# Attention on a graph: the product that spreads queries to edges, in two float32r halves instead of one fp32 product

## The chip, the cores and the metric

The kernel runs on one core of one Trainium2 chip. The time is the device time of a run in microseconds. The profile shows one execution, taken by the hardware profiler.

## What is computed

Eight layers over a graph of 3,125 nodes and 53,125 edges (sorted by destination), 256 features, each added to the stream x. The change is in the first, a graph attention with 8 heads of 32:

```
q = (nfeat @ Wq.T).reshape(n, HEADS, HEAD_DIM) / SCALING
k = (nfeat @ Wk.T).reshape(n, HEADS, HEAD_DIM)
v = (nfeat @ Wv.T).reshape(n, HEADS, HEAD_DIM)
attn = jnp.einsum('ehd,ehd->eh', k[src], q[dst])
attn = attn + attn_bias
m = jax.ops.segment_max(attn, dst, num_segments=n)
a = jnp.exp(attn - m[dst])
s = jax.ops.segment_sum(a, dst, num_segments=n)
a = a / s[dst]
out = jax.ops.segment_sum(v[src] * a[:, :, None], dst, num_segments=n)
return out.reshape(n, FEAT) @ Wo.T
```

The other layers are a small mixture of experts (it runs beside the attention, node tile by node tile), graph convolutions and larger expert layers.

## The kernel before

Nodes are cut into T = 25 tiles of P = 125. As edges are sorted by destination, the edges of a node tile lie together; each tile gets a window of WC = 18 chunks of 128 edges. A chunk's keys and values are gathered by source node with one indirect DMA from POOL (`gathered`, L1736), six chunks (PC) to a buffer `kv`; there are seven such buffers, three to a tile, and a gather waits for the fifth before it.

The queries of a tile are not gathered. They are a 125x256 matrix `q` (`queries`: two matmuls with `wq`, then a copy on ACT with the scale, L1987), and an edge's query is picked by a matmul: the one-hot matrix of a chunk, nodes by edges (`oht_f`, stationary), times `q` (moving) gives the queries of 128 edges in PSUM (`qx`, L2006 in `logits`). Two chunks fill a PSUM bank, and DVE multiplies the keys in `kv` by it (L2008). After six chunks DVE sums over each head (L2009). The one-hots come as a broadcast row of node numbers in bf16 (`oht`), which DVE compares with the partition's number (L1991); ACT casts them to the type of the matmul (L1995), six chunks at a time, into three buffers, one for each call of `logits` of a tile.

Then follow for each tile: the exponentials and their sums (`sums_of`), the weights (`weights_of`), values times weights on DVE (L2043 in `weighted`) and the sum over the edges of each node, again a matmul with one-hots, in fp32 (`acc`, L2050; its one-hots are cast by ACT at L2048), the division (`normed`), a transpose and the output projection. A loop over tiles interleaves these for three tiles: `now` (logits), `before` (weights, sums, projection) and `after` (loads, one-hots, queries). Between the parts `beside` does a step of the small expert layer (its matmuls are recorded at L300, in the tile `tr` above all).

Loads of a tile (`asked`): the one-hot rows `oht`, the transposed normalized nodes `lt_t` (L1972), and the edge biases `eb_t` (L1974), all on SP's queue, in pools with two buffers.

The order of instructions on each engine is not the order of the code: a planner in the compiler places each instruction by its place in the code and by an estimated time of its inputs, at compile time. At run time each engine takes its instructions in that fixed order, and waits come from semaphores. So an instruction that waits holds back all that stands behind it on its engine.

Later in the kernel the graph convolutions use a product in two float32r halves already: `halves` splits a matrix into a high half (ACT, L2355 or L2358) and the rest (DVE, L2356 or L2359), and `block_pass` multiplies both with a matrix of counts and adds in PSUM (L2418); L2516 transposes both halves by a matmul with an identity.

Of the kernel before, what the change touches and what calls it, by code (L numbers as in the profile page):

```python
# [10 lines left out]
F32 = mybir.dt.float32  # L11
F32R = mybir.dt.float32r
I32 = mybir.dt.int32
BF16 = mybir.dt.bfloat16
AF = mybir.ActivationFunctionType
ALU = mybir.AluOpType
# [6 lines left out]
N, D = 3125, 256  # L23
P, T = 125, 25
# [11 lines left out]
H, HD = 8, 32  # L36
# [12 lines left out]
WC, PC = 18, 6  # L49
# [21 lines left out]
def gnn_ffn_kernel(ctx: ExitStack, tc: tile.TileContext, a, out: bass.AP):  # L71
    nc = tc.nc
# [32 lines left out]
    def move(queue, to, of):  # L105

        queue.dma_start(to[:SPREAD], of[:SPREAD])
        return queue.dma_start(to[SPREAD:], of[SPREAD:])
# [185 lines left out]
    def product(ps, terms, bias=None):  # L294

        last = len(terms) - 1
        if bias is not None:
            nc.tensor.matmul(ps, ones_h[:bias.shape[0], :ps.shape[0]], bias, start=True, stop=False)
        for i, (l, r) in enumerate(terms):
            nc.tensor.matmul(ps, l, r, start=(bias is None and i == 0), stop=(i == last))  # L300
# [1401 lines left out]
    def attention(windows, experts):  # L1702
# [11 lines left out]
        with ExitStack() as es:  # L1714
# [16 lines left out]
            def gathered(at):  # L1731


                kv = rows_tile()
                for c in range(PC):
                    got = nc.gpsimd.indirect_dma_start(  # L1736
                        out=kv[:, c, KO:], out_offset=None, in_=kv_d,
                        in_offset=bass.IndirectOffsetOnAxis(ap=src_i[:, at + c:at + c + 1], axis=0))
                    if len(under_way) > 4:
                        tc.add_manual_dep(got.ins, under_way[-5].ins.name, data_dep, reason="in turn")  # L1740
                    under_way.append(got)
                nc.vector.memset(kv[:, :, KO - 1:KO], 1.0)
                return kv
# [3 lines left out]
            pool = setup.enter_context(tc.tile_pool(name="att_in", bufs=2, reuse_waits="tile"))  # L1747
# [210 lines left out]
            pool = es.enter_context(tc.tile_pool(name="att_s", bufs=2, reuse_waits="tile"))  # L1958
# [6 lines left out]
            def asked(t):  # L1965
                s = Tile()
                s.t, s.kv = t, begun if t == 0 else []
                s.oht = pool.tile([P, WC, 128], BF16, name="oht")
                move(nc.sync, s.oht.rearrange("d c e -> d (c e)"), turned_d[t * WC:(t + 1) * WC, :].rearrange("(o c) e -> o (c e)", o=1)
                     .to_broadcast([P, WC * 128]))  # L1970
                s.lt = pool.tile([128, 2, P], F32, name="lt_t")
                nc.sync.dma_start(s.lt, lt_d[:, :, t, :].rearrange("k f p -> f k p"))  # L1972
                s.eb = pool.tile([128, H, WC], F32, name="eb_t")
                nc.sync.dma_start(s.eb, eb_d[:, t])  # L1974
                return s
# [6 lines left out]
            def queries(s):  # L1982

                ps = psum.tile([P, D], F32, name="sm")
                product(ps, [(s.lt[:, k, :], wq[:, k, :]) for k in range(2)])
                s.q = pool.tile([P, D], F32, name="q")
                nc.scalar.activation(s.q, ps, AF.Copy, scale=float(HD) ** 0.5)  # L1987

            def one_hot_turned(s):
                v = s.oht.rearrange("d c e -> d (c e)")  # L1990
                nc.vector.tensor_scalar(v, v, pcol[:P], None, ALU.is_equal)  # L1991
                s.oht_f = []
                for c0 in range(0, WC, PC):
                    s.oht_f.append(pool.tile([P, PC, 128], F32, name="oht_f", bufs=3))
                    nc.scalar.copy(s.oht_f[-1], s.oht[:, c0:c0 + PC, :])  # L1995
                s.l = pool.tile([128, WC, H], F32, name="l")

            def logits(s, p):

                if p == len(s.kv):  # L2000
                    s.kv.append(gathered(s.t * WC + p * PC))
                kv = s.kv[p]
                for c0 in range(0, PC, 2):
                    ps = psum.tile([128, 2, D], F32, name="qx", bufs=2)
                    for c in range(2):
                        nc.tensor.matmul(ps[:, c, :], s.oht_f[p][:, c0 + c, :], s.q, start=True, stop=True)  # L2006
                    k_ = kv[:, c0:c0 + 2, KO:VO]
                    nc.vector.tensor_mul(k_, k_, ps)  # L2008
                nc.vector.tensor_reduce(  # L2009
                    s.l[:, p * PC:(p + 1) * PC, :],  # L2010
                    kv[:, :, KO:VO].rearrange("p c (h d) -> p c h d", h=H), AX.X, ALU.add)
# [59 lines left out]
            def projected(s):  # L2071
                po = psum.tile([P, D], F32, name="sm")
                product(po, [(s.at[:, k, :], wo[:, k, :]) for k in range(2)])
                nc.vector.tensor_add(x[:, s.t, :], x[:, s.t, :], po)

            now, before = asked(0), None
            one_hot(now)
            one_hot_turned(now)
            queries(now)
            more = experts()  # L2080

# [4 lines left out]
            for t in range(T + 1):  # L2086
                def beside():
                    if t % 4 == 1 and t < 16:
                        next(more_biases[t // 4], None)
                    more.step(t - 1)  # L2090

                after = asked(t + 1) if t + 1 < T else None
                if now:
                    logits(now, 0)
# [10 lines left out]
                if after:  # L2105
                    one_hot_turned(after)
                    queries(after)
                beside()
                if now:
                    logits(now, 1)  # L2110
# [4 lines left out]
                if now:  # L2115
                    logits(now, 2)
# [613 lines left out]
```

## Time and profile before

| | |
|---|---|
| median of 9 runs | 3242.23 us (3238.78 to 3247.43) |
| the profiled execution: its own time, its span | 3237.36 us, 3235.6 us |
| mean granted TensorE clock | 0.973 |
| attention stage, first qx to last tile's `deg` | 98 to 860 us |
| PE / DVE / ACT / POOL busy from 95 to 861 us | 710.0 / 575.8 / 255.3 / 483.4 us |
| DMA share and rate from 95 to 861 us | 0.65, 184 GB/s |
| L2050 acc, 900 records | 215.4 us, 394 ns mean |
| L2008 DVE kv times qx, 225 | 150.7 us, 680 ns mean |
| L1995 ACT cast oht_f, 75 | 828 ns mean |

PE is the matmul engine, PEld its weight loads (they overlap with it), DVE the vector engine, ACT the scalar engine, POOL the engine that issues the gathers, SP the one that issues most other transfers. A matmul's duration of some 380 ns is its latency; matmuls are pipelined, so what one costs is the time from its start to the next one's start. In groups, "xN | a, b | c" is the number, the busy time in us, the mean ns of one, and the idle time of the engine just before them, with what ended it. In waits, "A <- B: a, n, m" is who waited for whom: us in total, times, and the longest.

### The profile page before, as it was taken

The numbers are of one execution on the slowest core, as the hardware profiler recorded it, in microseconds if no ns is written. First come the engines' busy times: TensorE is split into PE (matmuls) and PEld (weight loads), VectorE is DVE, ScalarE is ACT, GpSimd is POOL, SyncE is SP. The second block draws the span as 40 slices with busy tenths as digits, with TensorE's granted clock in tenths as the row PEclk, the third lists the DMA queues.
The fourth block names the chain that finished last, engine by engine and source line by source line (L and its number), as shares of the span: only waits on it lengthen the run. The fifth ranks groups of instructions, "written<-read, shape, count | busy, mean of one in ns | idle before, by whom it ended". The sixth has DMA issues, their size and how long they took to land.

```text
span 3235.6 us, 43324 instructions
## 1 busy us (share of the span) xinstructions
PE 3032.6 (94%) x15467; PEld 2383.2 (74%) x15467; DVE 1739.3 (54%) x4900; ACT 1092.4 (34%) x2135; POOL 705.5 (22%) x664
## 2 busy tenths in 40 slices
PE   6799999999988999999987999979999999999998
PEld 3577777677778898898875888858755555578867
DVE  5577878788798344246671222265532333464683
ACT  3233333333378233233322222234423232332221
POOL 1676676666000000001223333200000000000000
PEclk9799999999999999999998999989999999999999
DMA  6776676776269434444436666554200000033101
GB/s 190 219 214 187 196 197 176 197 201 173 64 229 293 120 95 118 106 113 110 120 105 181 180 201 193 145 150 106 78 12 12 15 20 12 9 106 105 44 1 41
DMA packets 262345, 407.04 MB, mean 126 GB/s; under 512 B 43449, under 2 KB 206951, under 8 KB 262116
## 3 DMA queue, kind: packets, MB, share of 16 engines
q1 hardware_dynamic: 195985, 247.92, 26.4%
q0 software_dynamic: 54832, 143.43, 16.5%
q10 hardware_dynamic: 11299, 12.78, 1.5%
q8 instruction: 126, 2.06, 0.3%
q14 instruction: 103, 0.84, 0.1%
HBM read 333.28 MB, written 70.70 MB: 125 GB/s over the span
## 4 chain that ended last, share of the span: by engine, by line
PE 66%; DVE 6%; ACT 2%; DMA 1%; issue 1%; POOL 0%; POOLq 0%; SPq 0%; ACTq 0%; DVEq 0%
PE agg L2418 22%; PE po L300 19%; PE hid_ps L300 16%; PE tr L300 2%; PE tr L2516 1%; PE tok L1574 1%; PE row L300 1%; DVE hc L316 1%; PE tr L284 1%; DVE hr L316 1%; PE acc L2050 1%; ACT h L1398 1%; DVE an L2307 1%; PE bt L2304 0%; PE bk L2288 0%
## 5 line engine op out<-in xcount | busy, mean ns | idle before, releaser
L2418 PE MATMUL agg<-cnt_f,hp 125*128 125x500 f32 (+1 forms) x3500 | 743.0, 370 | 25.3 <-ACT hp L2358 25.2
L2418 PEld LDWEIGHTS agg<-cnt_f,hp 125*128 125x128 f32 x3500 | 635.0, 189 | 106.6 <-ACT hp L2358 28.3
L1736 POOL DMA_INDIRECT kv<-kv_d,src_w x450 | 472.2, 1049 | 242.2 <-issue 106.5
L2396 ACT CAST cnt_f<-blk 125x500 fp32r<-125x500 bf16 (+1 forms) x435 | 245.5, 565 | 494.5 <-PE agg L2418 472.8
L2396 DVE CAST cnt_f<-blk 125x500 fp32r<-125x500 bf16 (+1 forms) x440 | 186.8, 426 | 232.5 <-PE agg L2418 193.9
L1398 ACT ACTIVATE h<-hid_ps,shift,scale 128x500 f32<-128x500 f32 (+1 forms) x224 | 161.8, 723 | 373.7 <-PE hid_ps L300 371.7
L2006 PE MATMUL qx<-q,oht_f 125*128 125x256 f32 x900 | 250.5, 406 | 26.0 <-DVE kv L2008 21.4
L1405 DVE TENSOR_TENSOR y<-po,wslot 125x256 f32<-125x256 f32 x200 | 84.8, 424 | 340.2 <-PE po L300 339.8
L1626 POOL MEMSET ost<- 128x512 f32 x1 | 0.5, 524 | 1042.6 <-PE row L300 1042.6
L2006 PEld LDWEIGHTS qx<-q,oht_f 125*128 125x128 f32 x900 | 170.2, 200 | 66.3 <-DVE kv L2008 33.1
L2050 PE MATMUL acc<-kv,oh_f 128*125 128x265 f32 x900 | 215.4, 394 | 1.1 <-ACT oh_f L2048 1.1
L300 PE MATMUL po<-wslot,h 128*125 128x256 f32 x800 | 203.0, 386 | 0.1
L300 PEld LDWEIGHTS po<-wslot,h 128*125 128x125 f32 x800 | 145.0, 187 | 75.3 <-ACT h L1398 27.0
L300 PE MATMUL hid_ps<-h,wslot 128*128 128x500 f32 (+1 forms) x448 | 194.5, 557 | 5.3 <-ACT h L1398 1.7
L1257 ACT ACTIVATE hid<-hid_ps,wslot 128x256 f32<-128x256 f32 x208 | 98.3, 474 | 296.2 <-PE hid_ps L300 296.2
L2050 PEld LDWEIGHTS acc<-kv,oh_f 128*125 128x125 f32 x900 | 171.3, 192 | 34.8 <-ACT oh_f L2048 1.5
L1102 POOL DMA_INDIRECT xs_d<-r_l,pos x50 | 59.2, 1184 | 610.6 <-DVE r_l L1098 597.5
L300 PE MATMUL hid_ps<-xe,wslot 128*128 128x256 f32 x832 | 189.1, 385 | 2.2 <-DVE xe L1246 2.2
L300 PE MATMUL hid_ps<-v_rows,wslot 128*128 128x500 f32 (+1 forms) x448 | 186.4, 537 | 0.0
L300 PE MATMUL po<-wslot,hid 128*128 128x256 f32 x832 | 184.5, 378 | 0.0
L2008 DVE TENSOR_TENSOR kv<-kv,qx 128x512 f32<-128x512 f32 x225 | 150.7, 680 | 50.9 <-PE qx L2006 26.8
L300 PEld LDWEIGHTS hid_ps<-xe,wslot 128*128 128x128 f32 x832 | 152.1, 192 | 34.1 <-ACT hid L1257 3.8
(519 smaller groups left out, 4650.6 us busy)
## 6 DMA issues: line engine op xcount, KB each, us to landing
wslot<-in_ex_W SPq DMA_DIRECT2D x52, 1024.0 KB
blk<-an_d SPq DMA_DIRECT2D x60, 546.9 KB
blk<-at_d SPq DMA_DIRECT2D x40, 546.9 KB
blk<-an_d SPq DMA_DIRECT2D x45, 410.2 KB
at_d<-ab SPq DMA_DIRECT2D x25, 683.6 KB
an_d<-an SPq DMA_DIRECT2D x25, 683.6 KB
oht<-turned_d SPq DMA_DIRECT2D x25, 504.0 KB
blk<-at_d SPq DMA_DIRECT2D x30, 410.2 KB
```

The source lines that it names most:

```text
L300: nc.tensor.matmul(ps, l, r, start=(bias is None and i == 0), stop=(i == last))
L316: return nc.vector.tensor_tensor(o.rearrange("p n (d w) -> p n d w", w=2), columns[:, :m].rearrange("p (d w) -> p d w", w=2).unsqueeze(1). ...
L1102: st = nc.gpsimd.indirect_dma_start(out=xs_d, in_=l2[:, i, :].bitcast(I32), in_offset=None, out_offset=bass.IndirectOffsetOnAxis(ap=self.p ...
L1257: nc.scalar.activation(hid[:, m, :], ps[:, :BLK], AF.Gelu, bias=c[:, 4 + m:5 + m])
L1398: nc.scalar.activation(dst[:, m, :c], ps[:, :c], AF.Relu, bias=shift[:, l, col:col + 1], scale=scale[:, l, col:col + 1])
L1405: nc.vector.tensor_add(y, po, bo)
L1736: got = nc.gpsimd.indirect_dma_start(out=kv[:, c, KO:], out_offset=None, in_=kv_d, in_offset=bass.IndirectOffsetOnAxis(ap=src_i[:, at + c: ...
L2006: nc.tensor.matmul(ps[:, c, :], s.oht_f[p][:, c0 + c, :], s.q, start=True, stop=True)
L2008: nc.vector.tensor_mul(k_, k_, ps)
L2050: nc.tensor.matmul(s.acc[:, :D + H + 1], of[:, c, :], kv[:, c, AO:VO], start=(p == 0 and c == 0), stop=(p == 2 and c == PC - 1))
L2396: to(f[:, :n, :], part[0][:, :n, m % MB, :])
L2418: nc.tensor.matmul(ps[f][:, :c], hp[:, m, k, f * 128:(f + 1) * 128], got[:, :c], start=(m == 0 and k == 0), stop=(m == T - 1 and k == 1))
```

## The change

`q` becomes a float32r tile with two parts: ACT writes the scaled query rounded to float32r (12 significant bits), and DVE writes the scaled query less that part, also in float32r. The one-hots are cast to float32r. For each chunk two matmuls with the same stationary one-hots add the two parts in PSUM. The tile `lt_t` has one buffer instead of two.

```diff
@@ asked
-                s.lt = pool.tile([128, 2, P], F32, name="lt_t")
+                s.lt = pool.tile([128, 2, P], F32, name="lt_t", bufs=1)
@@ queries
-                s.q = pool.tile([P, D], F32, name="q")
-                nc.scalar.activation(s.q, ps, AF.Copy, scale=float(HD) ** 0.5)
+                s.q = pool.tile([P, 2, D], F32R, name="q")
+                nc.scalar.activation(s.q[:, 0, :], ps, AF.Copy, scale=float(HD) ** 0.5)
+                nc.vector.scalar_tensor_tensor(s.q[:, 1, :], ps, float(HD) ** 0.5, s.q[:, 0, :].bitcast(F32),
+                                               ALU.mult, ALU.subtract)
@@ one_hot_turned
-                    s.oht_f.append(pool.tile([P, PC, 128], F32, name="oht_f", bufs=3))
+                    s.oht_f.append(pool.tile([P, PC, 128], F32R, name="oht_f", bufs=3))
@@ logits
-                        nc.tensor.matmul(ps[:, c, :], s.oht_f[p][:, c0 + c, :], s.q, start=True, stop=True)
+                        for k in range(2):
+                            nc.tensor.matmul(ps[:, c, :], s.oht_f[p][:, c0 + c, :], s.q[:, k, :],
+                                             start=(k == 0), stop=(k == 1))
```

## The prediction

> **What bounds the kernel now.** I began with the page's busy shares and slices, to see where the changed code runs and which engine is full there.
>
> ```profile
> PE 3032.6 (94%) x15467; PEld 2383.2 (74%) x15467; DVE 1739.3 (54%) x4900; ACT 1092.4 (34%) x2135; POOL 705.5 (22%) x664
> ...
> L2006 PE MATMUL qx<-q,oht_f 125*128 125x256 f32 x900 | 250.5, 406 | 26.0 <-DVE kv L2008 21.4
> ```
>
> The changed product (L2006) has 900 records, though the code asks for 25 tiles x 18 chunks = 450: an fp32 product leaves two records. By its tile view it runs from 98.2 to 836.7 us, which is the attention stage. The windows view says what is full in the middle of that stage (columns: PE, PEld, DVE, ACT and POOL busy, granted clock, DMA share, GB/s).
>
> ```profile
> 300.00:780.00 480.00, 454.17 (x2500) 359.63 (x2499) 375.38 (x790) 170.03 (x355) 320.69 (x304) 0.99 0.68 191
> ```
>
> PE is busy 95% of it, DVE 78%. POOL's 67% leaves out the 0.30 us that its timeline shows between two gathers: 1.25 us each x 18 = 22.5 us of a tile. The `deg` copies that end the tiles follow one another at 29.6 us (147.4 to 859.7 us, 24 steps). PE leads, but two engines stand close behind.
>
> A busy PE is not the same as a PE that decides, so the chain of waits came next. The page's chain breaks off at a gather at 787 us. I walked back by the same rule from the accumulation that ends at 770.5 us, which reaches the start of the program. Of 98.2 to 770.5 us it gives PE 362.0 us (acc 119.6, the neighbouring layer's tr 87.4, qx 80.6), gathers in flight 68.0, their issue on POOL 54.5, DVE 71.5. Before 300 us qx has only 11.7 of that, and the gathers 83. From 787 us on the page's own chain has 5.9 us of qx, and between the two I take 2 us by the same density: **88 us of qx on the chain**, of 900 x 216 ns = 194 us that PE spends on it.
>
> **The rates.** The chain in order of time and the PE timeline give the pace of matmuls that follow one another (start us, us, what):
>
> ```profile
> 475.81 1.89 PE L2006 MATMUL qx<-q,oht_f 125*128 125x256 f32 x8
> 477.54 1.03 PE L300 MATMUL sm<-wo,at 128*125 128x256 f32 x4
> ...
> 1126.34 22.69 PE agg L2418 x100
> 1149.03 1.73 PE tr L2516 x16
> 1150.76 6.96 PE po L300 x32
> 1157.72 17.16 PE agg L2418 x100
> ```
>
> Eight qx records go from 475.81 to 477.54: 216 ns each, so one fp32 product is 432 ns. L2418 is float32r in this kernel and has one record a matmul: 3,500 records for 5 passes x 7 groups x 25 blocks x 4. It takes 227 ns at 500 columns and 172 ns at 376. L2516, float32r at 126 columns, takes 108 ns with a weight load before each.
>
> **The change, part by part.** *Products.* 450 fp32 products of two records become 900 float32r matmuls: no fewer records or weight loads. No row has 256 float32r columns. The line through 500 and 376 (0.444 ns a column) gives 172 - 120 x 0.444 = 119 ns. From below, the 126-column row bounds it (108), from above the 376-column row (172). I take 119, since weight loads that limit at 108 would be covered. PE is relieved of 900 x (216 - 119) = 87 us (40 to 97); the old chain gets shorter by 88 x 97/216 = **39.5 us** (18 to 44). If instructions keep their order and lengths, the chain's saving is all that can be gained, as the rest of this path stays.
>
> The Trainium skill's "TensorE: Matmul & The Clock Gate", section "Back-to-back issue gap", has N/2.4 + 2.5 ns, 109 ns here, and by that the chain would give 43.6 us. The same section expects some 81 ns at 128 columns with weight loads where this trace has 108 at 126, so I stay with the rows.
>
> *The low half on DVE.* 25 new scalar_tensor_tensor of 125x256 out of PSUM. The same operation with the same output stands at L2356:
>
> ```profile
> L2356 DVE SCALAR_TENSOR_TENSOR hp<-v,hp x50: 416/425/428, 1208.8 to 1455.4; 125x256 fp32r<-125x256 f32 x50
> ...
>   ACT hp L2355: 6.3, 23
> ```
>
> 25 x 0.424 = 10.6 us of DVE. It reads SBUF there; L2060, which reads PSUM at this size, has 421 ns, so that is no difference. DVE has 71.5 of 672 us of the chain, 11%, which makes 1 us; all of it on the path makes 10.6. I take 3, since DVE is nearly full in some tiles (28.1 us of 780 to 810).
>
> *Its wait.* The instruction waits for ACT's high half, which waits for PE's product with wq. Until now DVE waited for neither. What is queued behind it on DVE, the kv products that PE and the gathers wait for, waits too. In L2356 the same pair (ACT high, DVE low) lost 6.3 us in 50, 0.13 each: 3.2 us for 25. The upper end is ACT's own wait for that product today:
>
> ```profile
> ACT q L1987 <- PE sm L300: 35.4, 13, 6.5
> ```
>
> 2.7 us a time, for 25 tiles 68 us. I take 3.2, the row of the same pair.
>
> *Casts on ACT.* `oht_f` and the high half are written as float32r instead of fp32. L2396 (ACT, 500 elements to float32r) has 609 ns; with 268 more at 0.83 (the page's 565 ns mean mixes in 375) that is 831, what L1995 takes today. L2355 has 417 ns where L1987 has 384: 25 x 0.03 = 0.8 us on ACT, which is busy 35% of the stage. At nothing; without that cover, 0.8.
>
> *One buffer for `lt_t`.* SP's load of the next tile now waits until the wq product of the tile before has been read. The last such load is issued at 733.3 us and read at 789.9, a lead of 57 us; the product before it ends near 754, which leaves 36 us for a transfer of 125 KB. Behind it in SP's queue stand the `eb_t` load, which already waits on its own buffer (282.6 us for DVE's L2015, in the queue's waits), and the `oht` loads, last issued at 789.4. At nothing; if a delayed `oht` load followed from it, DVE's present wait for such loads (24.6 us in 6) prices one at 4 us.
>
> *The clock.* Between 160 and 800 us the granted clock falls to half seven times, for 3.4 us each. Three of these follow a stretch of over 3.4 us without a matmul; one such pair:
>
> ```profile
> 440.00:443.50 3.50, 0.00 (x0) 0.00 (x0) 2.85 (x7) 1.99 (x4) 3.00 (x2) 1.00 0.37 112
> 444.20:447.60 3.40, 3.02 (x9) 1.66 (x7) 3.40 (x14) 1.40 (x3) 2.55 (x3) 0.51 0.68 187
> ```
>
> Half clock for 3.4 us costs about 1.7 us. A PE that is done sooner waits more: ten more such stretches would be 17 us, none is possible as well; I take two, 3.4 us, as nearer to the seven in 25 tiles of today. "TensorE: Matmul & The Clock Gate", Part 1, ties the drop to an idle window of some 3.4 us, a rule that speaks against relieving an engine that then waits; by it, waits that stay shorter would cost nothing and the sum would be 33 us. Four of the seven drops here follow shorter gaps, so the rule doesn't cover them.
>
> **The sum.** 39.5 - 3 - 3.2 - 3.4 = 30 us off the profiled execution. Its own time was 3237.4 us with a span of 3235.6; the median of nine runs is 3242.2, so 3212 beside the median. What follows the stage starts from its last accumulation (the chain goes on from there through the one-hots of the next stage), so the gain is passed on whole. Over 44 us would take another order of the instructions, and that the planner may give one, since their lengths change, is the largest unknown.
>
> **The rivals.** *PE's whole relief arrives*, because the order adapts: 87 - 7 = 80 us, **3162**. For it: 3.5 us a tile off 29.6 leaves 26.1, above DVE's 23.6 (375.4/480 x 29.6 + 0.4) and POOL's 22.5. Against: today's leader gets to 29.6 only with two followers at 23; three nearly equal ones don't overlap perfectly, and the first 200 us belong to gathers.
>
> *The next one takes over at once*: nothing, **3240** (within 6.5 us of before). For it: six chunks cost DVE three products and a reduction (page: 680 ns; 1746 ns in the by-shape groups), 3 x 0.68 + 1.75 = 3.8 us, and PE 12 x 0.216 = 2.6, so inside the logits DVE is already slower. Against: PE fills the rest of these stretches with acc and tr, and the chain goes through those.
>
> *DVE waits for q* (slower): the wait above at 2.7 us in every tile, 68 us, less the 22% in which DVE idles anyway, 53; 53 + 10.6 - 39.5 = +24, **3266**. It decides from (39.5 - 10.6)/25 = 1.2 us of uncovered wait a tile. For it: ACT really waits so in 13 of 25 tiles, and DVE is strict in its order. Against: the wq product is computed ahead of its use, and the pair at L2355 and L2356 waits little.
>
> That the change doesn't do what it says, a float32r matmul at 256 columns costing 172 ns, leaves 18 - 10 = 8 us, 3234: the upper end of the forecast.
>
> **How the numbers follow.** Forecast (3195 to 3235): 0.45. All of PE's relief (3150 to 3195): 0.17. Nothing: 0.13. Slower by the wait, or by an unlucky new order: 0.25. A measurement of this kernel can tell 0.2%, 6.5 us, from no change. Faster 0.45 + 0.17 = 0.62, same 0.13, slower 0.25. The forecast's own range is 3195 to 3235; that for 8 in 10 reaches half way into both outer cases, 3165 to 3262.
>
> **What would show it.** Right: qx at some 119 ns start to start with 900 records; the tiles' pace at 28.4 us from 300 to 780 us; PE's busy share down, DVE's up. Wrong: qx at 170 ns or more; DVE idle before the new line for ACT over 30 us in all; stretches of half clock in most tiles; a pace under 27 us (the order adapted) or over 29.6.

## The result, and the profile after

| | before | after |
|---|---|---|
| median | 3243.22 us (33 runs) | 3255.82 us (11 runs, 3248.68 to 3261.86) |
| ratio, 95% interval | | 1.0036 [1.0026, 1.0046] |
| profiled execution: own time, span | 3237.36, 3235.6 us | 3252.75, 3250.9 us |
| mean granted clock of the span | 0.973 | 0.950 |
| last `deg` of the attention | 859.9 us | 868.0 us |
| first agg of the next stage | 1036.4 us | 1048.6 us |

The kernel became slower by about 12 us. The page of the changed kernel: busy time of each engine, the granted clock in 40 slices, and the group of the changed product; below it the granted clock of the kernel before.

```profile
PE 3004.1 (92%) x15467; PEld 2378.9 (73%) x15467; DVE 1745.7 (54%) x4925; ACT 1090.4 (34%) x2135; POOL 719.8 (22%) x664
...
PEclk9689899898898999999997999989999999999999
...
L2009 PE MATMUL qx<-q,oht_f 125*128 125x256 f32 x900 | 190.9, 347 | 31.8 <-DVE kv L2012 23.4
```

```profile
PEclk9799999999999999999998999989999999999999
```

PE is less busy, with the same number of records, and qx is cheaper: the forecast's first signs hold. The line of the clock is the one to look at. The second to the eleventh digit are the attention. Before they were a 7 and nine 9s; now they are a 6, five 8s and four 9s. The windows view of the stage before, of the stage after and of its middle (columns: PE, PEld, DVE, ACT, POOL busy, granted clock, DMA share, GB/s):

```profile
95.00:860.00 765.00, 709.41 (x3792) 556.28 (x3792) 574.83 (x1183) 255.27 (x538) 483.36 (x460) 0.95 0.65 184
```

```profile
95.00:868.00 773.00, 677.27 (x3791) 548.16 (x3789) 580.24 (x1205) 253.15 (x538) 496.60 (x459) 0.87 0.65 182
300.00:780.00 480.00, 431.98 (x2479) 350.61 (x2478) 375.78 (x798) 166.19 (x352) 326.82 (x296) 0.91 0.68 188
```

From 300 to 780 us PE is busy 22 us less than before, and the clock is 0.91 where it was 0.99. The other columns moved by 3% at most. The stage, from 95 us to its last `deg`, divided by what PE did (worked out from the trace: PE's busy time, that part of it in stretches of half clock, and the same work counted at full clock, which is busy less half of that part):

```
          stage   PE idle   PE busy   of it at half clock   work at full clock
before    764.9     55.5     709.4          61.3                 678.8
after     773.0     95.7     677.2         164.3                 595.1
```

The change took 84 us of work from PE. Half clock gave back (164.3 - 61.3) / 2 = 51 us, and idle time 40 us, so the stage came out 8 us longer. Half clock came in 26 stretches (201 us in all) after and 10 (69 us) before.

What one drop looks like: PE's timeline (start us, us, what, idle before it and what ended it), and the windows view of the same microseconds, cut where the clock changes.

```profile
360.60 1.19 PE L2009 MATMUL qx<-q,oht_f 125*128 125x256 f32 x8
362.10 0.74 PE L2009 MATMUL qx<-q,oht_f 125*128 125x256 f32 x4 [0.31 <-DVE kv L2012]
364.23 0.62 PE L2037 MATMUL sm<-m,oht 125*128 125x8 bf16 x18 [1.40 <-DVE m L2033]
...
367.42 3.63 PE L2009 MATMUL qx<-q,oht_f 125*128 125x256 f32 x13
```

```profile
360.81:364.22 3.41, 1.72 (x12) 1.41 (x12) 3.00 (x7) 0.00 (x0) 0.67 (x1) 1.00 0.60 190
364.22:367.63 3.41, 3.40 (x29) 2.92 (x28) 1.68 (x5) 2.44 (x5) 0.00 (x0) 0.50 0.42 153
367.63:371.05 3.42, 3.42 (x15) 3.11 (x15) 2.52 (x6) 1.76 (x7) 0.00 (x0) 0.50 0.23 58
371.05:374.46 3.41, 3.41 (x19) 2.71 (x18) 3.41 (x3) 1.38 (x6) 0.00 (x0) 1.00 0.27 108
```

In the first window PE waits 0.31 and 1.40 us for DVE, and streams for half of the time. In the next two its clock is half: 13 qx take 3.63 us, where eight took 1.19. No gap here is near 3.4 us. None of the 25 drops in the changed kernel's attention follows a gap of over 3.4 us; the longest idle time up to a drop, in the window before it, is 2.24 us.

### The profile page after: what moved, and what is told of

It reads as the page before. It is cut to its first block, busy times and chain, and to the rows that moved or that the text cites. A ratio compares the mean times of both kernels' runs of the same rounds, so it can differ in the third digit from the quotient of the medians.

```text
span 3250.9 us, 43325 instructions
## 1 busy us (share of the span) xinstructions
PE 3004.1 (92%) x15467; PEld 2378.9 (73%) x15467; DVE 1745.7 (54%) x4925; ACT 1090.4 (34%) x2135; POOL 719.8 (22%) x664
## 5 line engine op out<-in xcount | busy, mean ns | idle before, releaser
L1736 POOL DMA_INDIRECT kv<-kv_d,src_w x450 | 482.0, 1071 | 235.4 <-issue 109.3
L2054 PE MATMUL acc<-kv,oh_f 128*125 128x265 f32 x900 | 235.2, 419 | 4.0 <-DVE kv L2047 4.0
L2009 PE MATMUL qx<-q,oht_f 125*128 125x256 f32 x900 | 190.9, 347 | 31.8 <-DVE kv L2012 23.4
L2054 PEld LDWEIGHTS acc<-kv,oh_f 128*125 128x125 f32 x900 | 183.4, 206 | 42.5 <-DVE kv L2047 5.0
L2009 PEld LDWEIGHTS qx<-q,oht_f 125*128 125x128 f32 x900 | 147.7, 220 | 51.2 <-DVE kv L2012 28.4
```

The costliest lines, as they stand in the source:

```text
L1736: got = nc.gpsimd.indirect_dma_start(out=kv[:, c, KO:], out_offset=None, in_=kv_d, in_offset=bass.IndirectOffsetOnAxis(ap=src_i[:, at + c: ...
L2009: nc.tensor.matmul(ps[:, c, :], s.oht_f[p][:, c0 + c, :], s.q[:, k, :], start=(k == 0), stop=(k == 1))
L2054: nc.tensor.matmul(s.acc[:, :D + H + 1], of[:, c, :], kv[:, c, AO:VO], start=(p == 0 and c == 0), stop=(p == 2 and c == PC - 1))
```

## Experiments

Kernels were timed in turn with the kernel before on the same chip, and ratios are to it; a thousandth is 3.2 us. First: is it the number of products, the low half on DVE, or the clock?

**c1, one product; c2, three.** The loop over the halves, cut or lengthened. c1, shown here, leaves the low half (the part that DVE writes) out of the sum; c2 runs over (0, 1, 1) and so adds it twice.

```diff
-                        for k in range(2):
+                        for i, k in enumerate((0,)):
...
-                                             start=(k == 0), stop=(k == 1))
+                                             start=(i == 0), stop=(i == 0))
```

> Leaves out the second product of each chunk (the queries' low half is computed and not used), so 450 float32r matmuls less than the changed kernel, 54 us of PE. Clock theory (the gain is eaten by half clock, which comes when few columns stream through PE): the granted clock in the stage falls below the changed kernel's 0.87, to 0.80 to 0.85, and the time stays within 15 us of 3256. Rival, PE's work decides and something else was added on the path (DVE's low half, its wait): clock about 0.87, time 3256 less 45% of 54, some 3232. Rival, the new order of instructions: no forecast of the clock, time anywhere within 20 us of 3256.

> Adds the low half of the queries twice: a third float32r matmul a chunk, 450 more than the changed kernel, 54 us more of PE. Clock theory: the clock in the stage rises from 0.87 to 0.91 or more, and the time is not longer than the changed kernel's, 3235 to 3258. Rival, PE's work decides: 3256 + 24 = 3280 or more, with the clock as it was.

Measured: c1 3242.56 us, 0.9992 [0.9983, 1.0001]; c2 3269.47 us, 1.0068 [1.0055, 1.0081]. 450 products of 120 ns are 54 us of PE, and by the ratios 14 us of time from two to one and 10 us from two to three. In c1 the work at full clock fell to 548.6 us, the clock of the stage to 0.833 and idle time rose to 114.6 us; c2 has 648.4 us and 0.905. The less PE has to do, the lower its clock, and a cut in its work paid a quarter or a fifth of itself here. c1 came as the clock theory had it; c2's time lies between the two expectations (3258 and 3280) and decides for neither, though its clock rose.

**c3 and c4, the clock held up by fillers.** Sixteen bf16 matmuls of 240 columns a tile, whose results nobody reads, go into free columns of PSUM tiles: eight ahead of the sums, eight ahead of the weighted sum. c3 is the changed kernel with them, c4 the kernel before with them.

```diff
+            def fill(ps, n):
+                v = row_h.rearrange("p a b -> p (a b)")
+                for k in range(n):
+                    nc.tensor.matmul(ps[:, 272:512], ones_h[:, :ps.shape[0]], v[:, 64 * k:64 * k + 240], start=True, stop=True)
...
+                fill(ps, 8)
...
+                fill(s.acc, 8)
```

> The changed kernel with 16 bf16 matmuls of 240 columns a tile whose result nobody reads, 8 before the sums of the exponentials and 8 before the weighted sum, where PE often waits: 16 x 25 x 0.105 = 42 us more of PE. Clock theory: the clock in the stage goes from 0.87 to 0.95 or more, half clock stretches from 26 to under 12, and the time falls to 3205 to 3240. Rival, DVE's low half and its wait: the clock may rise, the time stays at 3256 or grows up to 20 us. Rival, order: no gain, 3250 to 3275.

> The same fillers in the kernel before. Clock theory: its 10 half clock stretches of the stage (69 us) become about 5; it loses some 31 us to half clock, of which a part before 200 us stays; 42 us more PE work stands against it: 3225 to 3255. Rival, PE's work decides: 3242 + 42 x 0.6 = 3267.

Measured: c3 **3217.90 us, 0.9909 [0.9894, 0.9924]**; c4 3237.70 us, 0.9983 [0.9971, 0.9995]. The page and the middle of the stage of c3:

```profile
PEclk9699999999999999999988999999999999999999
```

```profile
300.00:780.00 480.00, 455.60 (x2855) 375.96 (x2854) 394.17 (x830) 174.34 (x366) 333.87 (x310) 0.96 0.71 197
```

And some fillers (L2020) in PE's timeline of c3, between pieces of real work:

```profile
378.99 0.68 PE L2020 MATMUL acc<-row_w,ones_h 128*125 128x240 bf16 x5
379.61 1.13 PE L300 MATMUL sm<-wo,at 128*125 128x256 f32 x4
380.57 0.37 PE L2020 MATMUL sm<-row_w,ones_h 128*125 128x240 bf16 x2
380.78 1.02 PE L300 MATMUL tr<-lt,wslot 128*128 128x250 f32 x4
```

With 400 more instructions PE ends the attention 33 us earlier than in the changed kernel (stage 740.0 us). The clock is back at 0.96, and DVE and the gathers get more done in the same 480 us, as their higher counts show. The clock of c3's whole stage is 0.931, with 13 stretches of half clock, short of the 0.95 and the 12 that were expected. By the ratios the fillers bring 41 us to the changed kernel and 5.5 to the kernel before. But fillers change two things: the clock, and the planner's order.

**d1, DVE's part in the kernel before; d4, the changed kernel without it.** d1 adds the low half's instruction, which nobody reads, and the single `lt_t` buffer to the kernel before. d4 has no such instruction; its second product reads a tile of zeros, so the low half is left out.

```diff
+                nc.vector.scalar_tensor_tensor(s.q2[:, 1, :], ps, float(HD) ** 0.5, s.q,
+                                               ALU.mult, ALU.subtract)
```

```diff
-                            nc.tensor.matmul(ps[:, c, :], s.oht_f[p][:, c0 + c, :], s.q[:, k, :],
+                            nc.tensor.matmul(ps[:, c, :], s.oht_f[p][:, c0 + c, :], (s.q, no_low)[k],
```

> The kernel before with the changed kernel's DVE instruction (the low half is computed, and not used) and its single lt_t buffer; the product stays fp32. Clock theory: the clock in the stage stays at 0.93 or more, time 3240 to 3252. Rival, DVE's low half and its wait cost what the relief of PE gives: 3265 or more. Rival, an unlucky order of the planner for any program with this instruction: also 3255 or more, with the clock at 0.93 or more.

> The changed kernel without DVE's instruction: the second product of each chunk reads a matrix of zeros, so the low half of the queries is left out. Clock theory: nothing changes in what PE streams, the clock stays at 0.85 to 0.90, and only DVE's 10.6 us and its 12.1 us of waits go, of which at most half is on the path: 3243 to 3258. Rival, DVE's low half and its wait hold the gain back: 3215 to 3230.

Measured: d1 3246.13 us, 1.0017 [1.0008, 1.0027]; d4 3245.72 us, 1.0016 [1.0007, 1.0025]. The instruction with its wait costs some 5 us put in, and (1.0036 - 1.0016) x 3243 = 6.5 us taken out. Without it the changed kernel is still slower than before: DVE is not the cause.

**d2, fillers of 8 columns; d3, more fillers.** d2 has c3's instructions, each filler 8 columns wide instead of 240. d3 has ten more fillers a tile, ahead of the transposes of the weighted sum.

```diff
-                    nc.tensor.matmul(ps[:, 272:512], ones_h[:, :ps.shape[0]], v[:, 64 * k:64 * k + 240], start=True, stop=True)
+                    nc.tensor.matmul(ps[:, 272:280], ones_h[:, :ps.shape[0]], v[:, 64 * k:64 * k + 8], start=True, stop=True)
```

```diff
+                wide = psum.tile([128, 512], F32, name="sm")
+                fill(wide, 10)
```

> The changed kernel with the same 16 matmuls a tile as c3, in the same places, but of 8 columns instead of 240: almost the same order of instructions, almost no columns streamed. Clock theory: the clock stays near the changed kernel's 0.87 (0.85 to 0.90) and the time at 3245 to 3265. Rival, c3 was faster through its order: 3210 to 3230 with a low clock.

> c3 with 10 more fillers a tile before the transposes of the normalized rows, where c3's PE still waits up to 1.6 us and two of three of its last half clock stretches begin: 26 us more PE. Clock theory: the clock goes from 0.93 to 0.95 or more, time 3200 to 3218. Rival, PE's work decides: 3218 + 12 = 3230.

Measured: d2 3248.22 us, 1.0023 [1.0015, 1.0032], clock of the stage 0.875; d3 3265.03 us, 1.0080 [1.0066, 1.0094], clock 0.928. Narrow fillers don't lift the clock and bring little. d3 is a miss: its clock is nearly that of c3, yet by the ratios it is 55 us slower. Its instructions come in a very different order; the planner had ten more to place. c1 to d4 stand under the same doubt, for each came in an order of its own.

So the order had to be held. The next kernels take the order of PE, DVE, ACT and POOL from the trace of another kernel, by a dependence without a wait between each two neighbours on an engine:

```diff
+        for engine, packed in GIVEN.items():
...
+            for a_, b_ in zip(of, of[1:]):
+                tc.add_manual_dep(traced[engine][b_], traced[engine][a_].name, dep, reason="in turn")
```

**e1 (d2 in the order of c3), e2 (the changed kernel in the order of before), e3 (the kernel before in the order of the changed one), e4 (c4 in the order of c3).**

> d2 (the changed kernel with 16 matmuls of 8 columns a tile) with the order of every instruction of the attention on PE, DVE, ACT and POOL held to that of c3 (16 of 240 columns): the two differ in the columns that stream and in nothing else. Clock theory: the clock in the stage 0.90 or less against c3's 0.93, the time 3235 to 3260, at least 20 us over c3. Rival, c3's order was lucky: 3210 to 3225.

> The changed kernel with the attention's instructions held to the order of the kernel before (the two products in the place of the one; the low half before the first kv product that started after ACT's q in the profile of before). Clock theory: the clock falls below 0.92 in this order too, and the time is 3230 to 3255. Rival, the planner's new order cost the gain: 3200 to 3220.

> The kernel before (one fp32 product, two lt_t buffers) in the order of the changed kernel. Clock theory: 87 us more PE work than the changed kernel, but a clock of 0.93 or more: 3250 to 3275. Rival, the changed order costs the time: 3280 or more, as the chain would give 3256 + 40. If neither order nor PE's work decides: 3240 to 3250.

> c4 (the kernel before with 16 fillers of 240 columns a tile) held to the order of c3. If c3 is faster because PE is relieved while the clock stays up: 3245 to 3270, since the relief is undone. Rival, c3's order is what is fast: 3215 to 3230.

| | its order of | median | ratio [95%] | clock of the stage |
|---|---|---|---|---|
| e1 fillers of 8 columns | c3 | 3232.57 | 0.9967 [0.9951, 0.9984] | 0.899 |
| c3 fillers of 240 columns | c3 | 3217.90 | 0.9909 [0.9894, 0.9924] | 0.931 |
| e2 changed | before | 3248.89 | 1.0021 [1.0008, 1.0034] | 0.884 |
| after | after | 3255.82 | 1.0036 [1.0026, 1.0046] | 0.870 |
| e3 before | after | 3256.11 | 1.0037 [1.0023, 1.0051] | 0.954 |
| e4 before, fillers of 240 | c3 | 3249.87 | 1.0015 [1.0004, 1.0025] | 0.969 |

The stage of c3 and of e1, from 95 us to the last `deg` of each, as windows:

```profile
95.00:835.00 740.00, 681.79 (x4183) 561.32 (x4182) 581.12 (x1205) 252.92 (x538) 491.81 (x459) 0.93 0.68 190
```

```profile
95.00:847.00 752.00, 683.46 (x4184) 563.26 (x4184) 581.35 (x1207) 253.11 (x537) 489.92 (x460) 0.90 0.67 187
```

Four readings. First, e1 and c3 have the same instructions in the same order and differ in nothing but the width of the fillers. PE is busy for as long in both: what the narrow fillers save, half clock takes. But e1's PE idles more (68.5 us against 58.2), and the stage is 12 us longer. Over all runs the difference is 0.0058 x 3243 = 19 us (12 to 26 by the two intervals; the two kernels ran on two chips, each beside the kernel before). That is just short of the 20 us that were expected. Wider fillers are only more work, so what they bring comes through the clock. Second, e4 and c3 have the same order and the same fillers, and differ in the change alone (products, low half, buffer): (1.0015 - 0.9909) x 3243 = 34 us (28 to 40) for float32r, with the clock at 0.969 and 0.931. In the changed kernel's order without fillers the same step, e3 against the changed kernel, takes the clock from 0.954 to 0.870 and brings nothing (1.0037 and 1.0036). So the relief does reach the path, where the clock is held up. Third, d2 and e1 have the same instructions in two orders: 0.0056, 18 us. Fourth, e3 and e2 show that the changed kernel's order costs 12 us with fp32 products (0.0037), and 5 with float32r (1.0036 - 1.0021, whose intervals allow 0 to 10). The middle of the stage of e3 and of e2:

```profile
300.00:780.00 480.00, 449.38 (x2474) 356.10 (x2473) 372.37 (x781) 167.03 (x352) 315.20 (x297) 0.99 0.68 188
```

```profile
300.00:780.00 480.00, 434.93 (x2513) 351.86 (x2512) 381.01 (x810) 170.10 (x356) 321.69 (x305) 0.93 0.70 193
```

The clock follows the arithmetic: in the changed kernel's order, but with fp32 products, it is 0.99; in the order of before, but with float32r, it is 0.93.

The price of the clock can also be read within a kernel, since it differs from run to run. Three of the twelve runs of e1: 3222.89 us at a clock of 0.959, 3237.24 at 0.953, 3247.61 at 0.950. Clock lost is (1 - granted clock) x span of a run, and the slope is that of the span over it:

```
kernel                 runs   clock lost, mean us   slope   correlation
before (with e)          30          93.6            0.78      0.80
after                    13         164.4            0.55      0.75
c3                        4         108.5            0.68      0.94
e1                       12         143.5            0.71      0.96
e2                       12         156.7            0.84      0.91
all kernels, pooled     290                          0.64      0.76
```

By the pooled slope (0.64 +- 0.07; single kernels range from 0.26 to 1.05) the changed kernel's lost clock costs (164 - 93) x 0.64 = 45 us; by e1 against c3, 19 us for 35 us of clock, 0.54, it is 38. The slope is a correlation, the pair a trial, and they agree. The trial covers half of the 71 us of clock that the changed kernel lost; for the rest the price is an estimate from it.

**f1 to f3, g1 to g3.** What more fillers bring in c3's order (f1, g2), fillers in the order of before (f2, g1), DVE's instruction there (f3), and c3 once more (g3). These fell on two other chips, where the kernel before itself takes 3565 and 3547 us, so that only ratios on the same chip can be read.

Their edits are those shown, with another list of orders: f1 and g2 are d3's instructions in c3's order, f2 and g1 those of c3 in the order of before, f3 those of d1 in the order of before, and g3 is c3 unchanged.

> d3 (26 fillers a tile) held to the order of c3, its 10 further fillers just before the transposes. If d3's 3265 came from its order: the clock in the stage 0.94 or more and 3200 to 3225. If it came from PE's additional work: 3245 or more.

> The changed kernel in the order of the kernel before (e2) with c3's 16 fillers of 240 columns a tile, put right before the first matmul of the sums and of the weighted sum. Clock theory: order as before, PE relieved, clock in the stage 0.92 or more instead of e2's 0.88: 3210 to 3230. If PE's added work or DVE's low half holds the gain: 3245 or more.

> d1 (the kernel before with the low half computed on DVE and one lt_t buffer) held to the order of the kernel before, the low half where e2 has it: the cost of DVE's instruction and of its wait, with no new order and no change in PE's streaming. The clock as before, 0.95 or more. By the forecast's 3 + 3.2 us: 3244 to 3253. If that wait is what eats the gain: 3275 or more.

> The changed kernel with the 16 filler matmuls of c3 a tile, PE, DVE, ACT and POOL in the order of before. It stands against e2 (changed arithmetic, that order, no fillers: 1.0021, clock of the stage 0.884). Theory (the clock took the gain): the clock of the stage rises to some 0.93 to 0.95 and the ratio falls to 0.988 to 0.995. Rival (c3's gain came from its order alone): the clock rises, but the ratio stays at 1.000 to 1.006, since the fillers only add work.

> c3 with ten more fillers a tile ahead of the transposes of the weighted sum, the rest in the order of c3. d3, the same instructions in the planner's own order, had 1.0080. Theory (order was what cost d3, and more clock is still to be had): 0.985 to 0.993. Rival (the fillers themselves lengthen the path there): 0.996 to 1.008.

> c3 again, beside the two on the same chip: 0.989 to 0.993 if its gain (0.9909) is of the kernel; over 0.996 if it was of the chip or of the phase of the clock's windows.

| | median | ratio [95%] |
|---|---|---|
| f1, g2 more fillers, order of c3 | 3598.88, 3586.44 | 1.0091 [1.0077, 1.0106], 1.0104 [1.0080, 1.0128] |
| f2, g1 fillers, order of before | 3584.40, 3569.53 | 1.0047 [1.0034, 1.0061], 1.0055 [1.0035, 1.0075] |
| g3 fillers, order of c3 | 3554.57 | 1.0021 [1.0005, 1.0037] |
| f3 DVE's instruction in the kernel before | 3569.45 | 1.0013 [1.0002, 1.0024] |

The middle of the stage of g3, which is c3 again, and waits of its whole stage:

```profile
300.00:780.00 480.00, 344.13 (x1906) 280.09 (x1906) 263.64 (x559) 117.42 (x256) 208.59 (x204) 0.81 0.44 131
```

```profile
ACT oht_f L1997 <- remote: 130.8, 10, 16.7
...
DVE sums L2033 <- remote: 85.4, 8, 20.8
...
PE tr L300 <- issue: 67.8, 12, 12.0
```

By their counts all engines do some third less in these 480 us than in c3. The waits end on nothing that the trace shows ("remote", "issue"), up to 21 us at a time, on ACT, DVE and PE; c3's waits name no "remote" at all. What they are stays open. PE idles 325 us of this stage, and the clock is low in spite of the fillers; in such a stage they only add work. c3's gain was measured on one chip, on which the kernel before takes 3245 us, and it is not there on this one (1.0021, past the 0.996 that was named for "of the chip"); on how many chips it holds is open. What g1 and g2 were to settle, the clock's share at the order of before and whether more clock can be had, they don't: with f1 and f2 they are inconclusive. f3's 4 us agree with d1, and f3 holds the order.

## Why the prediction was wrong

*The rate and the relief* were right. qx goes 120 ns from start to start at full clock (119 forecast) with 900 records, and PE lost 84 us of work (87 forecast).

*What the relief is worth on the path* (39.5 us) agrees with e2, the changed arithmetic in the old order: it is 6.8 us slower, and its lost clock, (157 - 93) x 0.64 = 40 us, put aside leaves -33 us. The forecast's terms without the clock's are -39.5 + 3 + 3.2 = -33.3. That is closer than the numbers can be trusted: e2's time and the clock's price have some 4 us of uncertainty each, and no run had float32r products at the clock of before. The same working gives -44 us in the changed kernel's order (no difference to e3, with 68 us more clock lost) and -51 us in c3's (34 us faster than e4, with 27 us more clock lost). So the relief at an equal clock is worth some 33 to 51 us by this slope, and that it meets the forecast to the tenth is luck.

*The low half and its wait* (3 + 3.2 us) were right as a sum: 4 to 6.5 us in d1, d4 and f3. Of these only f3 holds the order. Its shares were not told apart. The view of the new line:

```profile
L1988 DVE SCALAR_TENSOR_TENSOR q<-sm,q x25: 372/419/425, 97.2 to 806.5; 125x256 fp32r<-125x256 f32 x25
...
  ACT q L1987: 9.2, 9
```

It takes the 0.42 us of L2356, and waits 9.2 us in all, nine times, where 3.2 was forecast and over 30 would have spoken for the rival.

*The casts and `lt_t`* cost nothing, as said: the casts take 827 ns (831 before), no engine waits for the `lt_t` load (SP's queue does wait for its buffer, 22.5 us in 15), and DVE waits 20.8 us for `oht` loads where it waited 24.6.

*The clock* is the step that failed. "I take two, 3.4 us, as nearer to the seven in 25 tiles of today": there were 26 stretches where 10 had been, most longer than one window of 3.4 us, 132 us more in all, which is 39 such windows and not two. They cost 38 to 45 us, about as much as the whole relief on the path (39.5). The upper end named there, ten more and 17 us, didn't hold it either, and "stretches of half clock in most tiles", which stood among the signs of being wrong, came true. The reason lies in how those drops were read. Three of seven followed a gap of over 3.4 us, and the other four were only called unexplained. They were the ones to learn from: in the same trace, drops follow windows in which little is streamed, whether or not there is a gap (the counts stand in the last section). The two float32r products of a chunk take 240 ns, the fp32 product kept PE at work for 432. The very quantity that was saved is the one that the clock follows, so the relief and the loss can't be costed apart.

*The order*, "the largest unknown", was put at nothing in the sum. It is worth 5 us here (0 to 10), to the bad side; the forecast's chance for slower included it.

Put together: -33 from the arithmetic, +40 from the clock in e2 and +5 from the order make +12, and the ratio's 0.0036 is 12 us. That sum closes by its making; what is independent in it is that the pair e1 and c3 gives the clock nearly the price of the slope.

*The rivals.* DVE's wait for q fell with its 9.2 us: the side was the one to which it gave a quarter, by another mechanism. "All of PE's relief" fell; the pace from the first `deg` to the last (144.2 to 867.8 us, 24 steps) is 30.15 us a tile, not 26, and over the 29.6 that was named as a sign against (before it is 29.68, which the prediction gave as 29.6). "The next one takes over at once" describes the outcome near zero, but not the cause: DVE's busy time in the middle is 375.8 us, as before, and c3 shows that the stage can go 33 us faster with the same DVE. A float32r matmul at 172 ns fell with the 120. The measured time, 3256 us, lies outside the forecast's 3195 to 3235 and within the range for 8 in 10 (3165 to 3262), near its upper end; as no case of the prediction had the clock as its cause, that it lies there is luck.

## What to carry to other kernels

Before taking work from a matmul engine that already idles in short pieces, cost the clock with the work: count what is streamed in each 3.4 us and see how many windows the change would bring under the limit (some 3,100 columns here, see below). Where that happens, a cheaper product can end slower, and cheap matmuls on data at hand, placed in the short waits, can bring the gain home (0.9909 against 1.0036 without, on one chip; nothing on another). Where a planner sets the order, any edit also buys a new order, worth up to 18 us here; a comparison of two versions means little until one is run in the other's order.

## What the runs showed of the hardware

*When the clock falls and returns.* The changes of the clock in a run lie on one grid of 3.4133 us, in both kernels to 2 ns over the whole attention. Counted on that grid: columns streamed by matmuls in a window, an fp32 record as two, since it takes 216 ns where float32r takes 120 at 256 columns. Each record counts in the window in which it starts. The windows from the first drop to some 865 us (c3's attention ends at 835, e1's at 847):

```
          stays at full clock       falls to half after it      returns to full after it
before    193 windows, from 2950     8, 1070 to 2700              9, from 3070
after     141 windows, from 2950    24, 1150 to 3280             25, from 3110
c3        182 windows, from 2620    11, 1310 to 3600             12, from 3730
e1        163 windows, from 2790    16,  490 to 3110             17, from 3150
```

A full window at full clock counts some 8,000 columns. Below about 2,600 none of these windows kept the clock, above 3,600 none lost it. Back it came only after 3,070 or more at half clock, and some windows with up to 3,700 did not bring it back.

Most of the width of these bands comes from records that lie across a window's edge. With each record's columns spread over its duration in the trace, the same count over the attention of all twenty kernels of this case (4,910 windows) leaves one limit for both directions: no window under 2,990 columns kept full clock or brought it back, and none over 3,290 was followed by half clock. So the limit is some 3,100 columns in a window, under four tenths of a full one. The window that began at 360.81 us holds 11 qx of 256 columns, 2,800.

The Trainium skill, "TensorE: Matmul & The Clock Gate", Part 1, has the free-running window of 3,413 ns, and the grid agrees with it. Its state table puts the drop after an idle window of about 3.4 us. Here the measurement decides: the window with PE busy for 1.72 of 3.41 us and no gap above 1.40 us lost the clock.

*One kernel, two times.* The kernel before took 3241 to 3245 us on three chips, 3547 and 3565 on two others, and for c3 the whole difference lies in the attention (1090.6 us there, 740.0 here), where engines stood still for up to 21 us for nothing that the trace names. c3's gain, sure on one chip of the first kind, was not there on the one of the second on which it ran. Whether the chips differ or something else was at work on them stays open.
